# Sums on ScalarE, scores and exponentials in halves, and small norm steps shared anew in a transformer kernel on one core

## The chip, the cores and the metric

The kernel runs on one core of one Trainium2 chip. A core has five engines that run their own instruction queues and wait for each other on semaphores: TensorE (PE in the profile; PEld is its loading of weights), VectorE (DVE), ScalarE (ACT), GpSimd (POOL) and SyncE (SP), which here only starts transfers. The metric is the time of one execution on the device, in microseconds (us), lower is better. Before the change the median of three runs was 2978.14 us (2974.05 to 2979.39).

## The reference

The input `x` is 32 sequences of 128 tokens with 128 features, with a context of the same size. First comes a cross-attention of 16 query heads and 4 key heads of size 8 with a time bias, then six layers, each of a local attention and a gated feed-forward part. Cut to what matters here:

```python
# cross-attention, once
x = x + xattn(layernorm(x), ctx, ...)          # softmax over 128 keys, 16 heads

for i in range(6):
    # local attention: 16 heads of 64, windows of 32 tokens that see themselves and the window before
    t = shift_tokens(x)                         # second half of the features from the token before
    q, k, v = split(t @ Wqkv[i])
    q = l2norm(q) * q_scale[i]; k = l2norm(k) * k_scale[i]
    q, k = rotate(q), rotate(k)                 # rotary tables with a scale
    sim = (bq @ bk2) * 8, masked                # 32 queries x 64 keys per window
    x = softmax(sim) @ bv2 @ Wo[i] + x
    # feed-forward
    t = shift_tokens(x)
    n = (t - mean) / sqrt(var + 1e-5) * g + b
    a, gate = split(n @ W1[i] + b1[i])          # 341 each
    x = (a * gelu(gate)) @ W2[i] + b2[i] + x
```

All of it is float32. The values and the output projection are folded into one matrix per head.

## The kernel before, in words

Tokens lie on the 128 partitions. Work is cut into *units* of one sequence (32 per layer) and *groups* of four sequences (8 per layer, `GB = 4`); the residual of a group stays in SBUF in `xt0` to `xt7`. `xgroup` and `xunit` do the cross-attention, `prep` prepares a layer's weights, `lgroup` starts a group of a layer, `unit` does its attention and `ffn` its feed-forward part.

The order of the instructions is not the order of the code. Every step is an operation given to `Sched.op` with a name, an engine, the buffers that it reads and writes, and a priority. `Sched.run` plans all of them ahead, before the program is written: it books each engine for the time that the table `COST` gives the name (engine, time that it occupies the engine, time until its result is there), moves priorities by the table `LATER`, keeps some buffers back by `KEEP`, and takes, on each engine, the first ready operation in order of priority. The order that comes out is written into the five queues and is fixed; on the chip each engine then runs its queue in that order and waits where an operand isn't there yet. A change in any entry of these tables reorders the whole program.

One `unit` runs like this, with the names in the plan and the lines of the profile:

- `qk` (four operations): query and key projections on TensorE. Each is three matmuls of 128x512 (`split3`, L438 to L440), the product of high and low parts in the faster float32 form. They go to one of five PSUM banks (pool `pj`).
- `sq` (L786, ScalarE) squares and `ss` (L801, VectorE) sums for the norms; `tab` (L792, VectorE) multiplies by the rotary tables and `add` (L798, GpSimd) completes the rotation.
- `newton` makes the reciprocal square roots of 32 norms: `mxs` (L405, GpSimd) puts a floor under the sums, `ln` and `ep` (L408, L411, ScalarE) take exp(-0.5 ln v), `ysq` (L415, ScalarE) squares it, and three steps `nw` on GpSimd (L420, L423, L426) refine it: times v, times -0.5 plus 1.5, times y. The same function serves the layer norm (`eps`, `lnf`, `epf`, `nwf`).
- `mul` (L815, GpSimd) scales, `tq` (L444, TensorE) transposes, `evq` (L820, ScalarE) copies the transposed heads to `qT`, four buffers per unit: two of queries and two of keys.
- `msk` (L857, ScalarE) puts the mask into the two PSUM banks of scores; `sc` (L852, TensorE) adds all scores of the unit, 128 small matmuls, as one operation. Bank 0 holds the even heads, bank 1 the odd ones.
- `mx` (L865, VectorE) takes maxima. For bank 1 `fold` (L867, TensorE) adds the negative maximum and `ex` (L869, ScalarE) is one exponential over 512 columns. For bank 0 `exb` (L873, ScalarE) is eight exponentials of 64 columns, each with its maximum as the bias.
- For both banks `sm` (L875, VectorE) sums the probabilities, `rl` (L876) takes the reciprocal, `pl` (L877, GpSimd) scales, `pt` (L879, VectorE) transposes in blocks.
- `y`, `yt` and `dm` (L831 to L834) make the projected values and move them into shape by a transfer; `av` (L892, TensorE, 56 matmuls) multiplies probabilities with them.

In `ffn`, `res` (L900) adds, `shift` moves token halves by two transfers, `st` and `ag` (L906, L910) take mean and variance, `newton` the reciprocal root, `nmr` (L915, VectorE, a scalar_tensor_tensor over 128x4) makes minus mean times the root, and `xn` (L920, ScalarE) normalizes. `ptn`, three `gate`, three `pa`, `w2` (L956) are TensorE's; `gel` (L937) needs another table on ScalarE, which is loaded for each group and loaded back (L254).

Ahead of the plan stands a start written by hand (L300 to L383): loads of constants and weights on the queues of SyncE and ScalarE, fills on GpSimd, and a few operations.

Of the kernel before, what the change touches and what calls it, by code (L numbers as in the profile page):

```python
# [16 lines left out]
P = 128  # L17
# [13 lines left out]
    qk=("PE", 0.76, 0.95), sq=("ACT", 0.53, 0.63), ss=("DVE", 0.6, 0.68), tab=("DVE", 1.14, 1.22), add=("POOL", 1.27, 1.3), ta=("DVE", .63, .72), adda=("POOL", 1.1, 6),  # L31
    mxs=("POOL", 0.25, 0.29), dmx=("DVE", 0.4, 0.48), dnw=("DVE", 0.34, 0.42), ln=("ACT", .2, .24), ep=("ACT", .2, .24), nw=("POOL", 0.24, 0.27),
    mul=("POOL", 1.01, 1.06), tq=("PE", 0.44, 0.68), evq=("ACT", 0.51, 0.61), evk=("ACT", .5, .62),
    y=("PE", 0.76, 0.95), yt=("ACT", 0.52, 0.62), dm=("SP", 0.58, 7.0), xph=("ACT", .6, .7), xpl=("ACT", .6, .7), dw=("SP", .62, 3.5), dr=("SP", .62, 4.5),
    msk=("ACT", 0.54, 0.63), sc0=("PE", .52, .75), sc1=("PE", .52, .75), mx=("DVE", 0.6, 0.68), fold=("PE", 0.31, 0.5), ex=("ACT", .51, .62), exb=("ACT", 1.62, 1.72),
    sm=("DVE", 0.6, 0.68), rl=("DVE", 0.13, 0.21), pl=("POOL", 1.02, 1.06), pt=("DVE", 0.62, 0.7), av=("PE", 1.95, 2.05), sc=("PE", 1.46, 1.6),
    res=("DVE", .63, .72), psh=("SP", 1.65, 3.5), st=("DVE", 0.79, 0.87), ag=("DVE", .35, .40), xn1=("POOL", 1.08, 1.1),
    eps=("POOL", .22, .26), lnf=("ACT", .22, .21), epf=("ACT", .22, .21), nwf=("POOL", 0.18, 0.24), xn=("ACT", 1.55, 1.65), nmr=("DVE", 0.4, 0.48), ysq=("ACT", .2, .24), xn2=("POOL", 1.08, 1.1),
    ptn=("PE", .46, .70), xnh=("ACT", .51, .62), xnl=("DVE", .60, .66), gate=("PE", 0.75, 0.95), gel=("ACT", 0.63, 0.7),
    pa=("PE", 0.73, 0.94), um=("DVE", 0.68, 0.76), w2=("PE", .67, .90), res2=("DVE", .63, .72), xo=("POOL", 1.3, 1.3),  # L40
    io=("SP", .62, 3.5), ldw=("SP", 0.5, 4.0),
# [10 lines left out]
LATER = dict(y=-0.75, xsc=-0.25, evk=-0.25, axl=-3.15, tab0=-2.45, tq3=2.8, pv=2.6, sq2=0.2, xex=1.55, ss1=1.2,  # L52
    mul3=-0.25, rl0=4.45, bip=-2.55, add3=3.2, pl0=0.8, bid=-0.4, ss2=-0.85, sq1=-0.9, xpa=0.25, tq2=1.45, mx0=3.2,
    sq3=0.45, wvp=2.75, ax=-0.7, qk3=-0.5, qk=-1.45, yt3=-1.55, tab2=-0.85, ysq=0.55, tq1=0.5, gate2=-3.4, um=-1.5,
    add2=2.2, w1c=0.35, fold1=1.5, gate=-0.25, mul2=2.55, dnw=-1.1, fold0=-2.5, y3=3, exb0=6.15, axh=0.8, mp=-1.0,
    eps=-1.05, pl1=5.15, add0=1.5, xat=-1.65, tq0=-2.25, nwf=0.25, pt1=2.15, msk0=1.45, xn1=4.2, um0=0.3, y1=3.8,
    sq0=-0.5, evq0=0.25, add1=-0.25, mul0=0.25, mkb=4.25, qk1=-0.35, pa2=-2.3, qkh=-1.2, mxs=-2.4, yt2=1.3, yt1=1.45,
    tab1=-1.7, td=1, evq1=-1.95, lnb=-2.25, ep=0.6, ss0=3.1, add=-0.5, y0=2.9, gate1=0.2, pa1=0.6, exb=-1.55,
    xsb=-1.6, mul=3.3, gel2=-0.9, mul1=-2, tab=2.8, ex=0.35, gel1=-0.5, msk=-2.35, pa=-0.5, rl1=0.5, dm2=-1.5,
    ss=4.05, dm0=0.25, ag=1.5, xo=4, qk0=-0.3, ln=-1.75, evq=0.25, sq=1.35, pa0=0.35, xst=-0.95, vt=0.6, ss3=-0.75,  # L60
    hil=-0.55, st=-0.8, tb=3, um2=1.6, nmr=3.45, gel0=0.5, xrl=-0.75, xev=-1.75, gate0=-1.2, yt0=1.75, rl=1.5,
    dm3=-1.9, av=3.35, lof=-1, gel=0.75, xnh=1.6, pwm=-1.0, pl=-0.25, yt=-0.9, sm=-0.25, res2=-0.25, res=-0.5,
    tbm=0.8, ldw=-0.5, pt=-0.9, wve=-1, sm1=-0.5, fold=-1.25, w1a=0.75, dm1=-1.7, sm0=1, lnf=-2.75, w1b=0.25, epf=1.1,
    xag=-0.75, tq=1.5, sc=1.5, pt0=-1.05, evq2=0.1, qkl=4, xpj=-0.7, xmx=2, xrs=-0.75, mx=1, dm=1.9, ex1=0.25,
    um1=-0.25, ml=-2, y2=0.95, evq3=-0.75, w2=1.5, nw=-0.75)

KEEP = dict(qk=0, y=0, gate=0, pa=1, xtr=0, xpj=1, pv=1, td=1, xsc=0, wvp=2, mp=2, bip=2, sc0=0, tq=0, ptn=0, ax=0,
    w2=3)
# [167 lines left out]
def body(ctx: ExitStack, tc: tile.TileContext, x, ctx_in, fside, mask_in, xWq, xWk, xWv, xWo, xtw,  # L236
# [73 lines left out]
    xt = [tl(f"xt{g}", [P, GB, 192]) for g in range(NG)]  # L310
    us = [tl(f"us{i}_", [P, 512]) for i in range(2)]
# [38 lines left out]
    nc.sync.dma_start(fs[:B, :], fside)  # L350
    wl = S.pools["raw"][0][2](F32)[:, 0:2 * P].rearrange("p (a n) -> p a n", a=2)
    nc.sync.dma_start(wl[:, 0, :], xWq)
    nc.sync.dma_start(wl[:, 1, 0:32], xWk)
    tw = tl("tw", [P, 1])
    nc.sync.dma_start(tw, xtw.partition_broadcast(P))
# [18 lines left out]
    for t in xt:  # L374
        nc.gpsimd.memset(t[0:1, :, 128:192], 0.0)
# [16 lines left out]
    def newton(names, pri, V, src, n, floor, eps, pool_, cols):  # L392
        v, y, t = [Buf(p) for p in pool_]

        def sl(b):
            return b.t[:, 0:n]
# [4 lines left out]
        def f0():  # L401
            if eps is not None:
                e.tensor_scalar(sl(v), cols(), eps, None, op0=ALU.add)  # L403
            else:
                e.tensor_scalar(sl(v), cols(), floor, None, op0=ALU.max)  # L405

        def f1():
            nc.scalar.activation(sl(y), sl(v), AF.Ln)  # L408
# [22 lines left out]
        S.op(names[3], f4, pri, [t, v], [t])  # L431
        S.op(names[3], f5, pri, [t], [t])
# [340 lines left out]
    def unit(l, g, j, w, G, pri):  # L773
# [89 lines left out]
        def soft(a):  # L863
# [6 lines left out]
            else:  # L870
                def pieces():
                    for i in range(8):
                        nc.scalar.activation(r8(pr)[:, i], r8(s)[:, i], AF.Exp, bias=mx.t[:, i:i + 1].bitcast(F32))  # L873
# [169 lines left out]
```

## Time and profile before

| | us |
|---|---|
| median of three runs | 2978.14 |
| the profiled execution | 2981.35 |
| its span, first to last instruction | 2979.2 |
| TensorE busy | 2874.9 |
| VectorE busy | 2616.2 |
| GpSimd busy | 2590.3 |
| ScalarE busy | 2504.6 |

The granted clock of TensorE was 0.987 of full speed over the span. A row of the timeline gives start, duration, engine, line, operation and tiles; durations on one engine overlap a little, so the time that an instruction takes from its engine is read from start to start. A wait names the engine that released it as far as the semaphores show it; "issue" stands where they show nothing. The first score matmul of a layer stands at 295 us; what is ahead of it is the cross-attention and the first preparations. The last matmul stands at about 2973 us.

### The profile page before, as it was taken

To read this page: it belongs to the slowest core of one execution; us is meant where nothing else is said; L and a number is where in the kernel's file an instruction comes from. 1 tells how busy PE (TensorE), PEld (TensorE's weight loads), DVE (VectorE), ACT (ScalarE), POOL (GpSimd) and SP (SyncE) were. 2 spreads that over 40 slices of the span, in tenths; PEclk is the share of its full clock that TensorE was granted. 3 is DMA by queue.
4 is the path that set the end of the run, shared out by engine and by line. 5 is a ranking of instruction groups with operands and counts; after the bars stand their busy time and mean duration, and the time that the engine had idled before them with its cause. 6 is when DMAs were issued, how large, how long until landed. Compare 5 with 4: busy or idle time off the path is not lost.

```text
span 2979.2 us, 115523 instructions
## 1 busy us (share of the span) xinstructions
PE 2874.9 (96%) x47695; PEld 2301.4 (77%) x47695; DVE 2616.2 (88%) x5203; ACT 2504.6 (84%) x6143; POOL 2590.3 (87%) x3238
## 2 busy tenths in 40 slices
PE   8999999999999999999999999999999999999997
PEld 5666777787877887777877888877788887777775
DVE  6778989998989998888998999988999998889884
ACT  6888888888888987888888888988888888888885
POOL 7768999898988998888988999989889998889893
PEclk8999999999999999999999999999999999999999
DMA  4101565656555565645556655556556556456555
GB/s 115 37 14 30 95 91 80 90 79 104 94 78 88 81 92 99 91 74 81 93 78 110 93 80 90 79 86 112 84 81 93 80 89 100 73 91 95 82 89 76
DMA packets 216881, 250.77 MB, mean 84 GB/s; under 512 B 90622, under 2 KB 111394, under 8 KB 216354
## 3 DMA queue, kind: packets, MB, share of 16 engines
q1 hardware_dynamic: 215922, 243.04, 51.5%
q8 instruction: 375, 6.14, 1.2%
q14 instruction: 152, 1.25, 0.2%
q10 hardware_dynamic: 432, 0.34, 0.0%
HBM read 25.31 MB, written 4.19 MB: 10 GB/s over the span
## 4 chain that ended last, share of the span: by engine, by line
PE 80%; DVE 6%; POOL 5%; ACT 4%; issue 4%; DMA 1%; POOLq 0%; SPq 0%; DVEq 0%; ACTq 0%
PE bank__68 L892 11%; PE bank__66 L852 4%; PE bank__67 L852 3%; PE bank__64 L438 3%; PE bank__62 L444 3%; PE bank__61 L444 3%; PE bank__63 L438 3%; PE bank__63 L444 3%; PE bank__65 L438 3%; PE bank__62 L438 3%; PE bank__65 L444 3%; PE bank__61 L438 3%; PE bank__64 L444 3%; PE bank__64 L439 3%; PE bank__64 L440 3%
## 5 line engine op out<-in xcount | busy, mean ns | idle before, releaser
L857 ACT COPY bank__66<-mask 128x512 f32<-128x512 f32 x192 | 123.6, 644 | 6.0 <-PE bank__66 L371 4.7
L857 ACT COPY bank__67<-mask 128x512 f32<-128x512 f32 x192 | 124.9, 651 | 0.9 <-PE bank__67 L371 0.9
L254 ACT ACT_TABLE_LOAD x48 | 61.6, 1283 | 0.9
L937 ACT ACT_TABLE_LOAD x48 | 61.6, 1283 | 0.9
L723 ACT ACTIVATE ysh__88<-ysh__88 128x512 f32<-128x512 f32 x64 | 40.1, 643 | 7.4 <-POOL ysh__88 L721 7.0
L900 DVE TENSOR_TENSOR xt<-bank__68,xt 128x512 f32<-128x512 f32 x48 | 32.8, 684 | 5.5 <-PE bank__68 L892 5.3
L723 ACT ACTIVATE wch__89<-wch__89 128x512 f32<-128x512 f32 x16 | 10.3, 646 | 8.0 <-POOL wch__89 L721 7.9
L960 DVE TENSOR_TENSOR xt<-bank__62,xt 128x512 f32<-128x512 f32 x11 | 7.6, 687 | 10.5 <-PE bank__62 L956 10.3
L960 DVE TENSOR_TENSOR xt<-bank__64,xt 128x512 f32<-128x512 f32 x9 | 6.2, 692 | 10.4 <-PE bank__64 L956 10.1
L960 DVE TENSOR_TENSOR xt<-bank__65,xt 128x512 f32<-128x512 f32 x12 | 8.3, 691 | 6.0 <-PE bank__65 L956 5.7
L967 POOL TENSOR_TENSOR raw__50871<-raw__50871,xt 128x512 f32<-128x512 f32 x1 | 1.3, 1261 | 14.0 <-DVE xt L960 14.0
L960 DVE TENSOR_TENSOR xt<-bank__63,xt 128x512 f32<-128x512 f32 x10 | 6.9, 688 | 7.5 <-PE bank__63 L956 7.3
L723 ACT ACTIVATE wch__90<-wch__90 128x512 f32<-128x512 f32 x16 | 10.1, 634 | 1.9 <-POOL wch__90 L721 1.9
L444 PE MATMUL bank__62<-cs,ysh__88 128*128 128x128 f32 x56 | 9.8, 302 | 0.6 <-ACT ysh__88 L723 0.6
L723 ACT ACTIVATE wch__92<-wch__92 128x512 f32<-128x512 f32 x16 | 10.2, 639 | 0.0
L723 ACT ACTIVATE wch__91<-wch__91 128x512 f32<-128x512 f32 x16 | 10.1, 633 | 0.0
L694 DVE TENSOR_TENSOR xt<-bank__68,xt 128x512 f32<-128x512 f32 x8 | 5.5, 685 | 4.9 <-PE bank__68 L692 4.9
L726 ACT COPY ysh__88<-bank__62 128x512 f32<-128x512 f32 x14 | 8.4, 599 | 1.6 <-PE bank__62 L444 1.6
L444 PEld LDWEIGHTS bank__62<-cs,ysh__88 128*128 128x128 f32 x56 | 6.7, 152 | 3.9 <-issue 1.7
L408 ACT ACTIVATE ny__51731<-nv__51729 128x4 f32<-128x4 f32 x1 | 0.2, 206 | 11.3 <-POOL nv__51729 L403 11.3
L444 PE MATMUL bank__61<-cs,xt 128*128 128x128 f32 x64 | 9.6, 273 | 0.0
L444 PE MATMUL bank__63<-cs,ysh__88 128*128 128x128 f32 x52 | 8.8, 295 | 0.4 <-ACT xh__1332 L766 0.2
(24257 smaller groups left out, 15643.2 us busy)
## 6 DMA issues: line engine op xcount, KB each, us to landing
xt<-xt SPq DMA_DIRECT2D x96, 112.0 KB
xt<-in_x SPq DMA_DIRECT2D x16, 128.0 KB
x_scratch<-xt SPq DMA_DIRECT2D x8, 256.0 KB
xt<-xt SPq DMA_DIRECT2D x96, 15.0 KB
stg__690<-in_L_ffn_Wo SPq DMA_DIRECT2D x1, 512.0 KB
stg__6126<-in_L_ffn_Wo SPq DMA_DIRECT2D x1, 512.0 KB
stg__19159<-in_L_ffn_Wo SPq DMA_DIRECT2D x1, 512.0 KB
stg__27202<-in_L_ffn_Wo SPq DMA_DIRECT2D x1, 512.0 KB
```

The source lines that it names most:

```text
L254: S.back = lambda: nc.scalar.preload_act_table_set("natural_log_exp_and_others")
L438: nc.tensor.matmul(pt, lh, rh, start=True, stop=False)
L439: nc.tensor.matmul(pt, lh, rl, start=False, stop=False)
L440: nc.tensor.matmul(pt, ll, rh, start=False, stop=True)
L444: nc.tensor.transpose(dst[:, k * P:(k + 1) * P], srcs[k], ident if eye is None else eye)
L723: S.op("xex", lambda: nc.scalar.activation(sm.t, sm.t, AF.Exp), pri, [sm], [sm], table="E")
L852: nc.tensor.matmul(s4[a][32 * c:32 * c + 32, half, wd, lo:64], q[r, c * P + 32 * wd:c * P + 32 * wd + 32], k[r, c * P + 32 * wd - 32 + lo: ...
L857: S.op("msk", lambda b=b: nc.scalar.copy(b.t, mask), pri, (), [b], k=a)
L892: nc.tensor.matmul(po.t[32 * wd:32 * wd + 32, j * P:(j + 1) * P], p5[a][:, half, wd, blk, :], ysh[0].t[:, u * 512 + h * P:u * 512 + (h + 1 ...
L900: S.op("res", lambda: nc.vector.tensor_tensor(xv(g), hv(po.t), xv(g), op=ALU.add), pri, [po, X[g]], [X[g]])
L937: S.op("gel", lambda: nc.scalar.activation(u.t[0:n], pg.t[0:n], AF.Gelu, bias=b1c.t[0:n, 1, i:i + 1]), pri, [pg, b1c], [u], table="G", k=i)
L960: S.op("res2", lambda: nc.vector.tensor_tensor(xv(g), hv(py.t), xv(g), op=ALU.add), pri, [py, X[g]], [X[g]])
```

## The change

- `soft`: for bank 0, each of the eight exponentials also writes the sum of its 64 probabilities (`accum_out`), and the operation `exb` becomes two of four pieces each; `sm` on VectorE stays for bank 1 alone.
- `scores`: the operation `sc` becomes two, one per half, each of 64 matmuls. The first needs `qT` 0 and 2, the second `qT` 1 and 3.
- `newton`, for the norms of the unit: `mxs` also multiplies by -0.5 and `ln` takes it back with its scale, so that after `ysq` and one `nw` step a single scalar_tensor_tensor `dnw` on VectorE, (t + 1.5) y over 128x32, takes the place of two steps on GpSimd.
- `ffn`: `nmr` goes to GpSimd, as two steps, `nmg` (times -1) and `nmr` (times the root).
- Start: the loads of `fside`, `Wq`, `Wk` and the weight of the time bias move from SyncE's queue to ScalarE's; the zeroing of `xt` on GpSimd stands ahead of the other fills; the load of `x` has a name of its own (`iox`) in the plan.
- `COST`, `LATER` and `KEEP` are new in many entries; the entries of changed or new operations are shown below.

```diff
@@ COST
-    ... qk=("PE", 0.76, 0.95) ... nw=("POOL", 0.24, 0.27) ... tq=("PE", 0.44, 0.68) ... y=("PE", 0.76, 0.95)
-    ... exb=("ACT", 1.62, 1.72) ... av=("PE", 1.95, 2.05), sc=("PE", 1.46, 1.6) ... nmr=("DVE", 0.4, 0.48)
+    ... qk=("PE", 0.72, 0.94) ... nw=("POOL", 0.31, 0.33) ... tq=("PE", 0.43, 0.66) ... y=("PE", 0.72, 0.94)
+    ... dnw=("DVE", 0.36, 0.44) ... exb=("ACT", 1.17, 1.3) ... av=("PE", 1.92, 2.02), sc=("PE", 0.72, 0.9)
+    ... nmr=("POOL", .18, .24), nmg=("POOL", .2, .26) ... iox=("SP", 1.1, 4.0)
@@ KEEP
-    pa=1, w2=3
+    pa=0, w2=0
@@ body, start
     xt = [tl(f"xt{g}", [P, GB, 192]) for g in range(NG)]
+    for t in xt:
+        nc.gpsimd.memset(t[0:1, :, 128:192], 0.0)
...
-    nc.sync.dma_start(fs[:B, :], fside)
+    nc.scalar.dma_start(fs[:B, :], fside)
...
-    nc.sync.dma_start(wl[:, 0, :], xWq)
-    nc.sync.dma_start(wl[:, 1, 0:32], xWk)
+    nc.scalar.dma_start(wl[:, 0, :], xWq)
+    nc.scalar.dma_start(wl[:, 1, 0:32], xWk)
...
-    nc.sync.dma_start(tw, xtw.partition_broadcast(P))
+    nc.scalar.dma_start(tw, xtw.partition_broadcast(P))
...
-    for t in xt:
-        nc.gpsimd.memset(t[0:1, :, 128:192], 0.0)
@@ newton
-                e.tensor_scalar(sl(v), cols(), floor, None, op0=ALU.max)
+                e.tensor_scalar(sl(v), cols(), floor, -0.5, op0=ALU.max, op1=ALU.mult)
...
-            nc.scalar.activation(sl(y), sl(v), AF.Ln)
+            nc.scalar.activation(sl(y), sl(v), AF.Ln, scale=-2.0 if big else 1.0)
...
         S.op(names[3], f4, pri, [t, v], [t])
+        if big:
+            S.op("dnw", lambda: nc.vector.scalar_tensor_tensor(sl(y), sl(t), 1.5, sl(y), op0=ALU.add, op1=ALU.mult), pri, [y, t], [y])
+            return y
@@ xgroup
-        S.op("io", lambda: halves(x, g, xo(g), False), base - 8, (), [X[g]])
+        S.op("iox", lambda: halves(x, g, xo(g), False), base - 8, (), [X[g]])
@@ unit
-        S.op("sc", scores, pri, [*qT, *sc], sc)
+        for half in range(2):
+            S.op("sc", lambda half=half: scores(half), pri, [qT[half], qT[2 + half], *sc], sc, k=half)
...
-                def pieces():
-                    for i in range(8):
-                        nc.scalar.activation(r8(pr)[:, i], r8(s)[:, i], AF.Exp, bias=mx.t[:, i:i + 1].bitcast(F32))
-                S.op("exb", pieces, pri, [mx, s], [pr], table="E", k=a)
-            S.op("sm", lambda: nc.vector.tensor_reduce(sm.t, r8(pr), axis=AX.X, op=ALU.add), pri, [pr], [sm], k=a)
+                def pieces(h):
+                    for i in range(4 * h, 4 * h + 4):
+                        nc.scalar.activation(r8(pr)[:, i], r8(s)[:, i], AF.Exp, bias=mx.t[:, i:i + 1].bitcast(F32),
+                                             accum_out=sm.t[:, i:i + 1])
+                for h in range(2):
+                    S.op("exb", lambda h=h: pieces(h), pri, [mx, s], [pr, sm], table="E", k=f"{a}{h}")
+            if a in FOLD:
+                S.op("sm", lambda: nc.vector.tensor_reduce(sm.t, r8(pr), axis=AX.X, op=ALU.add), pri, [pr], [sm], k=a)
@@ ffn
-        S.op("nmr", lambda: nc.vector.scalar_tensor_tensor(mv.t[:, :, 0], mv.t[:, :, 0], -1.0, r.t[:, 0:GB], op0=ALU.mult, op1=ALU.mult),
-             pri, [mv, r], [mv])
+        S.op("nmg", lambda: nc.gpsimd.tensor_scalar(mv.t[:, :, 0], mv.t[:, :, 0], -1.0, None, op0=ALU.mult), pri, [mv], [mv])
+        S.op("nmr", lambda: nc.gpsimd.tensor_tensor(mv.t[:, :, 0], mv.t[:, :, 0], r.t[:, 0:GB], op=ALU.mult), pri, [mv, r], [mv])
```

## The prediction

> **What bounds the kernel now.** I read the page first, then the windows by layer, then the waits of PE, then PE's timeline around a score block.
>
> ```profile
> span 2979.2 us, 115523 instructions
> ...
> PE 2874.9 (96%) x47695; PEld 2301.4 (77%) x47695; DVE 2616.2 (88%) x5203; ACT 2504.6 (84%) x6143; POOL 2590.3 (87%) x3238
> ...
> PE 80%; DVE 6%; POOL 5%; ACT 4%; issue 4%; DMA 1%; POOLq 0%; SPq 0%; DVEq 0%; ACTq 0%
> ```
>
> PE is busy for 96% of the span and carries 80% of the chain. The windows of two middle layers (span, busy PE, PEld, DVE, ACT, POOL) show that the helpers are close behind:
>
> ```profile
> 1186.00:1629.00 443.00, 428.04 (x7490) 349.55 (x7489) 396.64 (x643) 375.40 (x937) 391.94 (x487) 0.99 0.56 86
> 1629.00:2072.00 443.00, 437.25 (x7800) 356.02 (x7799) 408.11 (x658) 385.74 (x963) 403.02 (x501) 1.00 0.58 91
> ```
>
> PE's waits are small, and most name no releaser ("issue", in the middle of a row of ready matmuls); the largest inside the layers that do are single events of a microsecond:
>
> ```profile
> PE bank__68 L892 <- issue: 9.4, 15, 2.0
> ...
> PE bank__64 L956 <- issue: 6.4, 3, 3.6
> ...
> PE bank__67 L867 <- DVE mx__27187 L865: 1.4, 1, 1.4
> PE bank__62 L438 <- ACT yt__13943 L833: 1.3, 1, 1.3
> ```
>
> Busy time also hides what a change of work costs PE. In the timeline (start, duration), one projection (L438, L439, L440) follows another after 1511.10 - 1510.40 = 0.70 us. Next to transposes and scores it takes more:
>
> ```profile
> 1510.40 0.39 PE L438 MATMUL bank__64<-wch__19756,xh__24803 128*128 128x512 f32 x1
> ...
> 1511.10 0.40 PE L438 MATMUL bank__65<-wch__19765,xh__23812 128*128 128x512 f32 x1
> ...
> 1514.00 0.48 PE L438 MATMUL bank__63<-wch__11868,xh__24803 128*128 128x512 f32 x1
> ...
> 1514.88 0.21 PE L852 MATMUL bank__66<-qT__25698,qT__25669 64*32 64x32 f32 x1
> ...
> 1516.24 0.50 PE L438 MATMUL bank__62<-wch__19483,xh__24803 128*128 128x512 f32 x1
> ...
> 1517.04 0.60 PE L444 MATMUL bank__64<-cs,rt__25187 128*128 128x128 f32 x4
> ```
>
> The projection after transposes and before scores takes 0.88, the 128 score matmuls 1.36, the projection behind them 0.80. These prices repeat: sorting all starts on PE between 330 and 2880 us by kind of work and its two neighbours, the quarter point of "projection between projections" is 0.69, "after transposes" 0.78, "before scores" 0.78, "after scores" 0.80. Summed at these quarter points the work makes 2426 us; the stretch took 2548. Of the 122 us between them some 57 are the waits without releaser (PE's idle rows over the run), so **at most 65 us are waits for other engines**. That is all a better overlap can return there, besides the ends.
>
> **The change, step by step** (192 units of one sequence and layer, 48 groups of four; one unit takes (2975 - 295)/192 = 13.95 us).
>
> *Scores in halves.* No matmul is added, but in the built order the score blocks rise from 192 to 372: only 12 units keep their halves together. So PE changes work 180 times more. Price of one more block: its boundaries are 0.09 (before scores) and 0.10 (after) at projections, 0.08 to 0.13 at transposes; inside, the block takes 1.36 although its weight loads start within 1.17, so up to 0.17 drains once per block. From below: the boundaries alone, counted pair by pair in both orders with these prices (fewer projections now follow transposes or attention, which gives some back), make +31 us. From above: 180 x (0.19 + 0.17) = +65. I take **+45**, the middle, since the drain overlaps the next load partly. It lies on PE, so on the path.
>
> *How close the halves stand.* Between the last transposes that a half needs and the half itself, PE's order leaves this much other work (at the prices above): before, 1.75 us at the median; after, 1.07 for the second half. Transposes to scores needs about 0.42 (first eviction after its transposes start; median of the evictions that found ScalarE idle 0.69) + 0.60 (the eviction) + 0.2 (shortest gap eviction to scores) - 0.36 (the transposes themselves) = 0.86 to 1.13. So the second half waits whenever ScalarE is late: 0 to 0.25 us x 192 = 0 to +48. I take **+15**: the nearest rows (evictions that found ScalarE idle) only just fit. Behind a waiting half stand the other units' projections, all in PE's order.
>
> *ScalarE sums the even heads.* The reduce of L875 goes for one of two score banks: -192 x 0.60 (start to start) on VectorE, and its hop on the chain to the reciprocal. On ScalarE each of 1536 small exponentials writes a sum too:
>
> ```profile
> 1518.68 1.77 ACT L873 ACTIVATE pr__25915<-bank__66,mx__25892 128x64 f32<-128x64 f32 x8
> 1520.26 0.68 ACT L869 ACTIVATE pr__25939<-bank__67 128x512 f32<-128x512 f32 x1
> ```
>
> Eight pieces last 1.58, 0.197 each. What the sum adds isn't in this trace. From below 0; from above one more small instruction, 0.19 (L411, 128x32, start to start). The middle, 0.095, gives 8 x 0.095 = +0.76 a unit on ScalarE: 12.0 (13.85 less the idle rows before its instructions, 345 us over 188 units) becomes 12.8 of 13.95. Not on the path, but the evictions queue behind it. In pieces of four, other evictions can go between, which takes up to 0.8 off such a wait.
>
> *Small norm steps.* POOL loses two of four steps per unit (L423, L426: 0.25 and 0.29 start to start), 192 x 0.54 = -104, and gains two small ones per group, 48 x 0.4 = +19: -0.44 a unit. VectorE gets their place as one step with two SBUF inputs (dnw), and gives up nmr, of the same form. The rows of nmr say what that costs:
>
> ```profile
> 367.50 1.04 POOL L815 TENSOR_TENSOR rt__4859<-rt__4859,ry__5067 128x512 f32<-128x512 f32 x1
> ...
> 367.56 1.00 DVE L915 SCALAR_TENSOR_TENSOR nmv__5096<-nmv__5096,ny__5129 128x4 f32<-128x4 f32 x1
> ```
>
> It started just after a POOL instruction and ended with it (368.54, 368.56); of 48 such rows 42 last over 0.3 us, mean 0.80, the shortest 0.12. So dnw costs VectorE from 0.12 to 1.25 each (the longest POOL work, L798); I take 0.75 (nmr start to start): +144, against -115 for the reduce and -36 for nmr. **VectorE gains nothing.** Behind a blocked dnw stand the table products that free PE's banks; the four scalings of the unit on POOL wait for it, and in a quarter of the units POOL's order has only 0.2 us of work to put between, so about 0.2 of POOL's 0.44 comes back as waiting.
>
> The Trainium skill, "SBUF — State Buffer", section "Who interferes with whom", says that a VectorE instruction with two SBUF inputs contends with a GpSimd instruction that reads SBUF, and that whoever starts first holds the shared port for the whole instruction. The rows agree (1.00 beside POOL's 1.04). It speaks against dnw and for moving nmr; without it dnw would be 0.12 and VectorE 0.63 a unit lighter.
>
> What all this takes from PE's 65 us of waits: from above all of it (-65); from below nothing, or a loss if ScalarE's extra 0.76 counts more than POOL's net 0.24 (+20). POOL was the fullest helper and gets a little relief, ScalarE gets load: I take **-30**.
>
> *Start.* Four loads leave SyncE's queue for ScalarE's, whose issues (0.43 each) end before its first copy at 7.12; the zeroing of xt moves ahead of the other fills on POOL. Input rows could be asked for from about 1.2 instead of 4.68: at best -3.5; nothing, if the weights or the context then come last. I take **-3**. The cross-attention's order is new too, with the same blocks (75 runs of scores in both): 0, within 5 either way. The last 14 us are one chain of a group; minus and plus 0.2.
>
> Sum: 45 + 15 - 30 - 3 = +27 on the profiled execution's 2981.35, so 3008. That execution is 3.2 above the median of the runs (2978.14): 3005.
>
> **Rivals.**
> 1. *Faster: the waits on PE go.* The one mechanism is POOL: it is free for 0.44 us more per unit, so the rotated heads come earlier and PE finds its operands. For it: POOL is the fullest helper. Against: dnw hands the time back, and all waits are 65 us. Price: -65 (plus some -10 in the ends and the first 330 us), boundaries at their low end +31, start -3: -47, so 2931. It decides from the point where more than 55 of the 65 us go with boundaries at 45, or 35 with boundaries at 31.
> 2. *Slower by more: ScalarE or the second halves become the bound.* If the sum costs a whole small instruction, ScalarE reaches 12.0 + 1.5 = 13.5 of 13.95 and can't give evictions in time; or each second half waits 0.25. Boundaries 45 + 48 - 3, no relief: +90, so 3068.
> 3. *The parts cancel:* boundaries 31, waits -28, start -3: 2978.
> That the split isn't made is excluded: the order has 372 blocks.
>
> **How the numbers follow.** Forecast (2985 to 3030) 0.45; rival 2 (3030 to 3100) 0.16; rival 1 (2920 to 2970) 0.27; cancelling 0.12. No change is within 0.2% (6 us), about what a measurement can tell here. Slower: 0.45 + 0.16 = 0.61; of the cancelling case 0.11 stay within the 6 us and 0.01 falls below; faster 0.27 + 0.01 = 0.28. The likeliest is 3005, its own range 2985 to 3030. For 8 in 10 I go to 2945 below (leaving out a third of rival 1, 0.10) and 3060 above (half of rival 2, 0.08).
>
> **What would show it.** Boundaries: projections beside half blocks at 0.78 to 0.88 and half blocks near 0.7. VectorE busy not below 2600 and dnw near 0.8, ending with POOL's work. ScalarE's piece near 0.29. First statistics near 6 us instead of 9.60. I am wrong if PE's starts have fewer waits than 35 us in 330 to 2880, or if half blocks cost nothing at their edges.

## The result and the profile after

The changed kernel took **3067.64 us** (median of 4 runs, 3063.55 to 3070.35), the kernel before 2977.03 us beside it: a ratio of 1.0304, 95% interval 1.0286 to 1.0322. It is 90.6 us slower. The forecast was 3005, its range ended at 3060: right in sign, too low by two thirds of the loss, and the measured time lies above its range.

From the page of the changed kernel, its span, busy times and chain:

```profile
span 3065.6 us, 116691 instructions
...
PE 2917.4 (95%) x47695; PEld 2284.2 (75%) x47695; DVE 2564.3 (84%) x5155; ACT 2633.1 (86%) x7679; POOL 2537.7 (83%) x2950
...
PE 64%; DVE 12%; ACT 10%; POOL 6%; issue 3%; DMA 3%; SPq 0%; POOLq 0%; DVEq 0%; ACTq 0%
```

VectorE and GpSimd are each busy 52 us less than before and ScalarE 129 us more, but no helper is fuller than 86%. What changed is the chain: PE carried 80% of it and now 64%; VectorE's part has doubled and ScalarE's more than doubled. So PE waits more for results. In the stretch from 1629 to 2072 us PE is busy for 422.01 us and begins 7254 matmuls; before it was 437.25 and 7800, at the same granted clock of 1.00. (Over the whole span PE's busy time rose, from 2874.9 to 2917.4 us, though the durations of its rows sum to 12676 and 12665: the rows overlap less.) The waits of PE's weight loads, whose rows stand ahead of their matmuls, show new releasers: 4.7 us for L441 (four times, gelu L943 still reads the bank), single waits of 4.0 us for L447 (scaled heads, L818), 2.0 for L447 (eviction L823), 1.8 for L870 (maxima L868) and 2.4 for L898 (transposed probabilities, L885). Each is small; there are many. Summed over the layers of the profiled execution (from 35 us behind the first score block to 60 us ahead of the last, gaps over 0.15 us), the waits of PE's weight loads with a named releaser rose from 75 to 223 us, while those without one ("issue") fell from 200 to 145: 275 to 368, +92. The layers (first score block to last) took 2741 instead of 2646 us, +95; the start is 7.6 us shorter (first score block at 288.0 instead of 295.6).

That the two agree doesn't make the whole loss waiting. The weight loads' own busy time hardly moves (2301.4 us before, 2284.2 now), so whatever stretches PE's row stands between them as idle time, a change from one kind of matmul to another too. A half block of scores shows it:

```profile
1645.59 0.61 ACT L823 COPY qT__27410<-bank__63 128x512 f32<-128x512 f32 x1
...
1646.80 0.10 PEld L854 LDWEIGHTS bank__67<-qT__27410,qT__27395 64*32 64x32 f32 x1 [0.37 <-ACT sq__27429 L789]
```

The gap of 0.37 begins at 1646.43; the second of its two operands was there at 1646.20, and the squares named as the releaser are no operand of scores. Such a gap, 0.36 at the median, stands ahead of nearly every score block of both kernels: 191 gaps with 69 us before, 359 with 115 now.

The prediction's own method separates the two: price every step on PE by the quarter point of its times from start to start between the same two neighbours (here over both kernels' traces), and sum the prices over the sequence of the layers. **The price of PE's sequence rose from 2416 to 2469 us, +53; what the layers took beyond it rose from 134 to 177, +43.** (With the 5th or the 40th percentile in place of the quarter point: 55 and 42, 57 and 39; with prices from the traces of all kernels run here: 63 and 33.) So somewhat more than half of the loss is PE's own sequence, which changes work 180 times more, and the rest is waiting. Put down to the step that started late, the 43 are 19 ahead of folds, 12 ahead of transposes, 10 ahead of score blocks, 5 ahead of attention, and -3 in the others. The rest also holds the stops for which the profile shows no releaser; in PE's matmul rows they fell from 54 to 17 us, so the waits for named engines rose by more than 43.

Two edits as the trace shows them. ScalarE's sum is an instruction of its own, ACTIVATION_READ_ACCUMULATOR, behind each small exponential; a piece with its sum goes from start to start in 0.29 us instead of 0.20, as forecast. Here are two pieces in the first unit of the layers:

```profile
295.30 0.31 ACT L876 ACTIVATE pr__3968<-bank__66,mx__3950 128x64 f32<-128x64 f32 x1
...
295.50 0.20 ACT L876 ACTIVATION_READ_ACCUMULATOR pr__3968<-bank__66,mx__3950 128x1 f32 x1
295.59 0.31 ACT L876 ACTIVATE pr__3968<-bank__66,mx__3950 128x64 f32<-128x64 f32 x1
```

On PE, one half block of scores stands between two projections; 0.79 for the projection ahead of it, 0.74 for the half:

```profile
1646.01 0.39 PE L441 MATMUL bank__64<-wch__26773,xh__26646 128*128 128x512 f32 x1
...
1646.80 0.21 PE L854 MATMUL bank__67<-qT__27410,qT__27395 64*32 64x32 f32 x1
...
1647.54 0.50 PE L441 MATMUL bank__65<-wch__19718,xh__26646 128*128 128x512 f32 x1
```

The page's costliest groups on ScalarE are the copies of the mask, which still cost what they did, so its work as such isn't slower:

```profile
L859 ACT COPY bank__66<-mask 128x512 f32<-128x512 f32 x192 | 120.1, 626 | 5.4 <-DMA xt<-in_x 4.8
...
L859 ACT COPY bank__67<-mask 128x512 f32<-128x512 f32 x192 | 121.0, 630 | 1.5 <-PE bank__67 L373 1.1
```

They took a mean of 644 and 651 ns before, 626 and 630 now.

### The profile page after: what moved, and what is told of

Read it like the earlier page. It is cut to its first block, busy times and chain, and to the rows that moved or that the text cites. A ratio compares the mean times of both kernels' runs of the same rounds, so it can differ in the third digit from the quotient of the medians.

```text
span 3065.6 us, 116691 instructions
## 1 busy us (share of the span) xinstructions
PE 2917.4 (95%) x47695; PEld 2284.2 (75%) x47695; DVE 2564.3 (84%) x5155; ACT 2633.1 (86%) x7679; POOL 2537.7 (83%) x2950
## 4 chain that ended last, share of the span: by engine, by line
PE 64%; DVE 12%; ACT 10%; POOL 6%; issue 3%; DMA 3%; SPq 0%; POOLq 0%; DVEq 0%; ACTq 0%
PE bank__68 L898 9%; PE bank__66 L854 3%; PE bank__67 L854 3%; PE bank__64 L447 2%; PE bank__63 L447 2%; DMA xt<-xt 2%; PE bank__62 L447 2%; PE bank__61 L441 2%; PE bank__65 L441 2%; PE bank__62 L441 2%; PE bank__64 L441 2%; PE bank__63 L441 2%; PE bank__65 L447 2%; PE bank__61 L447 2%; PE bank__65 L443 2%
## 5 line engine op out<-in xcount | busy, mean ns | idle before, releaser
L859 ACT COPY bank__66<-mask 128x512 f32<-128x512 f32 x192 | 120.1, 626 | 5.4 <-DMA xt<-in_x 4.8
L859 ACT COPY bank__67<-mask 128x512 f32<-128x512 f32 x192 | 121.0, 630 | 1.5 <-PE bank__67 L373 1.1
L729 ACT COPY ysh__96<-bank__65 128x512 f32<-128x512 f32 x15 | 9.0, 598 | 2.8 <-PE bank__65 L447 2.3
L447 PE MATMUL bank__65<-cs,ysh__96 128*128 128x128 f32 x60 | 9.8, 288 | 0.8 <-ACT ysh__96 L726 0.7
L447 PE MATMUL bank__64<-cs,ysh__96 128*128 128x128 f32 x60 | 9.8, 288 | 0.1
L447 PEld LDWEIGHTS bank__65<-cs,ysh__96 128*128 128x128 f32 x60 | 7.0, 146 | 3.5 <-ACT ysh__96 L726 1.4
L447 PEld LDWEIGHTS bank__64<-cs,ysh__96 128*128 128x128 f32 x60 | 7.1, 146 | 3.4 <-ACT ysh__96 L726 2.4
L729 ACT COPY ysh__96<-bank__64 128x512 f32<-128x512 f32 x15 | 8.9, 596 | 0.7 <-PE bank__64 L447 0.7
```

The costliest lines, as they stand in the source:

```text
L447: nc.tensor.transpose(dst[:, k * P:(k + 1) * P], srcs[k], ident if eye is None else eye)
L729: S.op("xev", lambda: nc.scalar.copy(sm.t, pt.t), pri, [pt, sm], [sm])
L859: S.op("msk", lambda b=b: nc.scalar.copy(b.t, mask), pri, (), [b], k=a)
```

## The experiments

Differences are medians against the kernel before in the same job (2982 to 2984 us). Three theories stood first. A: the sums load ScalarE, and PE waits for its evictions. B: the new order, which the re-tuned tables make, leaves operands no time. C: dnw on VectorE is held by GpSimd.

### Single edits in the order of before

The sums alone, written to a spare tile, with VectorE's reduce kept (so their price without their gain; the cut `...` stands for the maxima):

```diff
-  nc.scalar.activation(r8(pr)[:, i], r8(s)[:, i], AF.Exp, bias=...)
+  nc.scalar.activation(r8(pr)[:, i], r8(s)[:, i], AF.Exp, bias=..., accum_out=spare[:, i:i + 1])
```

> The kernel before, in its own order, with each of the eight exponentials of the even heads also writing its sum, into a tile that nobody reads; VectorE's sums stay. Theory A (load on ScalarE: after the change each sum is an instruction of its own, 0.10 us start to start, 0.79 us a unit, and evictions come late for TensorE): a good part of the 90 us, 3020 to 3060. Theory B (the new order: the tables were re-tuned so that TensorE's operands come just in time): ScalarE had 1.84 us a unit free, so 2975 to 2995. Theory C (the norm step on VectorE, blocked by GpSimd): 2975 to 2990.

Measured 3029.21: **+46.9**, ratio 1.0155 (1.0139 to 1.0171). The page of this run:

```profile
PE 2896.1 (96%) x47695; PEld 2290.2 (76%) x47695; DVE 2618.5 (87%) x5203; ACT 2627.8 (87%) x7679; POOL 2598.5 (86%) x3238
...
PE 66%; ACT 12%; DVE 9%; issue 5%; POOL 5%; DMA 2%; SPq 0%; POOLq 0%; DVEq 0%; ACTq 0%
```

ScalarE is at 87% and yet its part of the chain goes from 4% to 12%.

dnw alone, in the place of GpSimd's last two steps (not shown: the factor -0.5 goes to `mxs`, and `ln` takes it back):

```diff
-  e.tensor_scalar(sl(t), sl(t), -0.5, 1.5, ...);  e.tensor_tensor(sl(y), sl(y), sl(t), op=ALU.mult)
+  nc.vector.scalar_tensor_tensor(sl(y), sl(t), 1.5, sl(y), op0=ALU.add, op1=ALU.mult)
```

> The kernel before, in its own order, with the two last norm steps of a unit on GpSimd replaced by the one step on VectorE, put where the second of them stood. A: VectorE gains 0.55 a unit, GpSimd loses as much: 2970 to 2990. B: the same. C: VectorE blocked for 0.55 a unit and the scalings late: 3010 to 3060.

Measured 2996.74: **+14.5** (1.0028 to 1.0063). The page of this run:

```profile
PE 2873.7 (96%) x47695; PEld 2295.5 (77%) x47695; DVE 2653.7 (89%) x5395; ACT 2515.4 (84%) x6143; POOL 2519.4 (84%) x2854
...
PE 61%; DVE 17%; POOL 8%; issue 6%; ACT 6%; DMA 1%; SPq 0%; POOLq 0%; DVEq 0%; ACTq 0%
```

GpSimd is 71 us lighter than before and VectorE 37 us heavier, but VectorE's part of the chain goes from 6% to 17%.

The start alone, with the layers' order unchanged:

```diff
+    for t in xt:  nc.gpsimd.memset(t[0:1, :, 128:192], 0.0)      # ahead of the other fills
-    nc.sync.dma_start(...)      # fs, wl (two), tw
+    nc.scalar.dma_start(...)
```

> The kernel before with the edits of the start alone: four constant loads on ScalarE's queue instead of SyncE's, the zeroing of xt ahead of the other fills; the layers' order is unchanged. The prediction gave this -3 (at best -3.5). The changed kernel reaches its first score matmul 7.6 us earlier than before (288.0 against 295.6), but there the cross-attention's order is new too. If the loads do it: 2973 to 2977 (-5 to -8.) If the earlier first scores came from the new order alone: 2980 to 2983, no change.

Measured 2983.44: ratio 1.0005 (0.9991 to 1.0019), **no change**. The first statistics did start at 6.56 instead of 9.60 us, but the first score block of the layers came at 295.1, almost as before (295.6): behind the cross-attention the gain is used up. So these edits alone don't give the 7.6 us of the changed kernel; its order there is another too.

The start and nmr in two steps on GpSimd:

```diff
-  nc.vector.scalar_tensor_tensor(mv0, mv0, -1.0, r, op0=ALU.mult, op1=ALU.mult)
+  nc.gpsimd.tensor_scalar(mv0, mv0, -1.0, None, op0=ALU.mult);  nc.gpsimd.tensor_tensor(mv0, mv0, r, op=ALU.mult)
```

> The kernel before with the edits of the start (which cost nothing, 2983.44 us) and nmr in two steps on GpSimd; the order is unchanged. If nmr on GpSimd is what was missing in the sum of the single edits (47 + 14 against 79): 2992 to 3005. If the edits act on each other when they come together: 2975 to 2988.

Measured 2997.62: **+14.0** (1.0034 to 1.0064), for 48 places. In the page GpSimd's part of the chain is 11% instead of 5%:

```profile
PE 2883.8 (96%) x47695; PEld 2301.0 (77%) x47695; DVE 2591.3 (86%) x5155; ACT 2504.6 (84%) x6143; POOL 2610.6 (87%) x3334
...
PE 68%; POOL 11%; DVE 7%; ACT 7%; issue 5%; DMA 2%; POOLq 0%; SPq 0%; DVEq 0%; ACTq 0%
```

### All of these together, in the order of before

> The order of before with every edit that it can take: sums on ScalarE (into a spare tile, the reduce kept), dnw on VectorE, nmr in two steps on GpSimd, the loads of the start. Score blocks stay whole. Theory L (the loss of the changed kernel is the load that the edits put on the helpers, in whatever order): the sum of the single runs, 47 + 14, less up to 7 for the start and with -10 to +5 for nmr, that is 2982 + 44 to 66, or more if the delays add up worse than singly: 3060 to 3080 would make it the whole loss. Theory O (much of the loss is that the changed kernel has another order, less well fitted): 3020 to 3048, so that 20 to 45 of the 86 us are left for the order with the halves.

Measured 3061.54: **+79.3** (1.0242 to 1.0280). The single edits sum to 47 + 14 + 14 = 75: they add up, and theory L holds for this order (VectorE's reduce of the even heads is kept here; the prediction put it at 115 us of VectorE's time). Its page:

```profile
span 3060.5 us, 116928 instructions
...
PE 2918.1 (95%) x47695; PEld 2295.3 (75%) x47695; DVE 2639.1 (86%) x5347; ACT 2633.6 (86%) x7679; POOL 2541.5 (83%) x2950
...
PE 46%; ACT 22%; DVE 16%; issue 7%; POOL 7%; DMA 1%; POOLq 0%; SPq 0%; DVEq 0%; ACTq 0%
```

PE's sequence costs as much as before here (+3 us); the layers' other 77 are waiting. The longest waits are those of the fold (here L872) behind the maxima (L870), up to 2.5 us. Between 330 and 2900 us all such fold waits sum to 41 us in 48 events, where before they were 7 us in 15. VectorE is hardly busier for it (2639 us, before 2616); its queue has dnw in it; that the score banks also reach it later from ScalarE is likely, but not shown. So a loss nearly as large appears without the changed kernel's order and without halves, but it is made of waits alone.

### The changed order without the loads

The changed kernel without the sums (the even heads stay unnormalized):

> The changed kernel in its own order without the sums on ScalarE; the reciprocal of the even heads is replaced by a small VectorE instruction on one column of the probabilities, so their normalization is left out. A: most of the loss goes, 2985 to 3020. B: 3045 to 3065, since the order is as tight as it was. C: 3055 to 3070.

Measured 3056.95: +74.7 (1.0230 to 1.0267).

The same, and dnw made an operation with one SBUF input:

> The changed kernel's order with both loads taken away: ScalarE writes no sums, and dnw is an operation with one SBUF input that no GpSimd work can hold (the even heads' normalization and the Newton step are left out, so its results are other numbers). Without the sums alone it took 3056.95. Theory L (load): with both away 2985 to 3010. Theory O (the order): 3035 to 3057, that is, at least 50 of the 86 us remain though the helpers have less to do than in the kernel before.

Measured 3045.93: **+63.7** (1.0192 to 1.0228). So sums and dnw, which cost 61 us in the old order, give back 27 in the new one, and 64 stay without them (nmr is still on GpSimd). Its page:

```profile
PE 2911.0 (96%) x47695; PEld 2287.0 (75%) x47695; DVE 2516.2 (83%) x5155; ACT 2515.9 (83%) x6143; POOL 2530.6 (83%) x2950
...
PE 71%; DVE 8%; POOL 7%; ACT 6%; issue 4%; DMA 3%; SPq 0%; POOLq 0%; DVEq 0%; ACTq 0%
```

No helper is fuller here than in the kernel before, where they were at 84 to 88% (ScalarE is busy 11 us longer, VectorE 100 and GpSimd 60 us less), and VectorE and ScalarE still take more of the chain than there (6% and 4%). Both theories are half right, and **the two parts don't add**: loads alone 79, the order nearly alone 64, both 91. In the layers of this run 53 us are the price of PE's sequence, which is that of the changed kernel, and 21 are waiting (changed kernel: 43).

Lighter helpers in the changed order, first VectorE alone:

```diff
-  nc.vector.tensor_reduce(ss..., sq.t.rearrange("p (h d) -> p h d", d=64), ...)
+  nc.vector.tensor_reduce(ss..., sq.t.rearrange("p (h d) -> p h d", d=64)[:, :, 0:32], ...)
```

> The changed kernel's order; the reduce of the squares (ss) sums only half of each head's columns, four times a unit (the norm of q and k is then another number). VectorE becomes about 4 x 0.28 = 1.1 us a unit lighter, and the statistics come earlier. If the order waits for VectorE above all (its share of the chain is the largest after PE's, 12%): 2990 to 3030. If the waits lie with all helpers alike, as much per us of work as the sums gave back on ScalarE (11 us for 0.76 a unit): 3045 to 3060.

Measured 3060.51: +78.6 (1.0234 to 1.0310). It isn't VectorE above all.

Then three helpers (half of the reduce on VectorE, half of the heads' scaling on GpSimd, no sums on ScalarE):

> The changed kernel's order with three helpers lightened: no sums on ScalarE (-0.76 us a unit), half of the squares' reduce on VectorE (-1.1), half of the scaling of the rotated heads on GpSimd (-2.0). Left out: the even heads' normalization and half of two other steps. If the 64 to 85 us that the order loses are waits for helpers: 2930 to 2990, since PE's own work per unit is no larger than in before. If PE's order itself is at fault (gaps that no faster helper closes, such as the distance between the second half and its transposes): 3030 to 3050.

Measured 3028.53: **+46.6** (1.0128 to 1.0195), just under the second expectation and far above the first. Its page:

```profile
PE 2913.4 (96%) x47695; PEld 2294.2 (76%) x47695; DVE 2367.4 (78%) x5155; ACT 2514.1 (83%) x6143; POOL 2218.9 (73%) x2950
...
PE 79%; DVE 7%; ACT 6%; issue 3%; DMA 3%; POOL 1%; SPq 0%; POOLq 0%; DVEq 0%; ACTq 0%
```

With VectorE at 78% and GpSimd at 73%, PE's part of the chain is back at 79%, but half of the loss is still there. It is no longer more waiting than before: what the layers took beyond the price of PE's sequence is 139 us here, 134 before, and the sequence costs 52 more. **Lighter helpers take back the waits; what stays is the longer sequence on PE.**

### Is it the tables?

The work of before, planned with all three new tables, with the new costs, with the new keep-rows, and with the new delays and keep-rows:

```diff
-LATER = dict(y=-0.75, xsc=-0.25, ...)      +LATER = dict(y=-0.35, iox=1.8, ...)
-KEEP = dict(..., pa=1, ..., w2=3)          +KEEP = dict(..., pa=0, ..., w2=0)
-COST: qk 0.76, sc 1.46, gate 0.75, ...     +COST: qk 0.72, sc 1.44, gate 0.72, ...
```

> The work of the kernel before (whole scores, whole exponentials, sums on VectorE, norm steps on GpSimd), planned with the new tables of costs, delays and kept buffers, the four changed operations booked as they are here. A and C: the tables alone are worth little, 2960 to 3000. B: the tables carry the loss, 3030 to 3090.

> The work of before, planned with before's delays and keep-rows, but with the changed kernel's costs (score block 1.44, small exponentials 1.62, as that work has them). The order of before with all three tables new took 3077.57 us, 95 above before. Theory B1 (the delays, LATER, carry the loss): the costs differ by 0.02 to 0.07 a step, so 2975 to 3000 here. Theory B2 (the costs carry it, because PE is planned 5% tighter): 3040 to 3080. Theory B3 (the tables fit one another, and any mixture loses, whichever part is exchanged): above 3010 here, and also in the two runs beside it.

> The work of before with before's costs and delays, and the changed kernel's keep-rows (the up-projection pa and the second matmul w2 no longer hold back for others: pa 1 to 0, w2 3 to 0). Theory B1 (delays): 2975 to 3000, since only where those matmuls stand may change. Theory B4 (keep-rows carry the loss): 3040 to 3080. Theory B3 (any mixture loses): above 3010.

> The work of before with before's costs, and the changed kernel's delays and keep-rows. Theory B1 (delays): 3050 to 3090, all of the 95 us that the three new tables cost. Theory B2 (costs): 2975 to 3010. Theory B3 (any mixture loses): above 3010, and then also in the run with the costs alone.

Measured: all three 3077.57 (**+95.3**), costs 3045.49 (**+63.4**), keep-rows 3059.89 (**+77.8**), delays and keep-rows 3046.56 (**+64.4**), each within 7 us either way. The chain of the run with the new keep-rows alone shows what happens to a work that is the same to the last instruction:

```profile
PE 2897.9 (95%) x47695; PEld 2295.4 (75%) x47695; DVE 2600.0 (85%) x5203; ACT 2503.8 (82%) x6143; POOL 2588.7 (85%) x3238
...
PE 59%; DVE 18%; ACT 8%; POOL 6%; issue 4%; DMA 4%; SPq 0%; POOLq 0%; DVEq 0%; ACTq 0%
```

VectorE and ScalarE are busy as before in us, and carry 26% of the chain, not 10%. PE's sequence costs as before in all four (-8 to +7 us), so these losses are waiting. No table carries the loss: B1, B2 and B4 would each need a harmless neighbour, and there is none, though the delays alone were not run. B3 holds. The other way round, the changed kernel's work with before's costs and delays (the keep-rows stay the new ones):

> All edits of the changed kernel (half score blocks, sums on ScalarE, dnw on VectorE, the loads), planned with before's costs and delays; the keep-rows are the new ones, and the rows that only the edits need (halves 0.73, pieces of four 1.17, the new norm steps) are the new ones too. Theory B (the new tables lose, the edits much less): 2990 to 3045, that is, below the changed kernel by 20 to 75, as the sums (+47) and dnw (+14) cost what they did in the order of before, less the 7 us of the earlier start. Theory A (the edits lose by ScalarE's load in any order, and the new tables are the best answer to them): 3065 or more. If it ends below 2975, the edits win by themselves and the new tables alone lose.

Measured 3140.41 (**+158.3**): a miss of theory B, which expected at most 3045. The new tables are not bad in themselves; they are worth 68 us to the changed work (158 against 91). In these runs a table is worth something only with the work that it was fitted to.

A slight change of the plan:

```diff
-rl=("DVE", 0.13, 0.21)
+rl=("DVE", 0.14, 0.22)
```

> The kernel before with a single planned cost raised by 0.01 us (the reciprocal rl, 0.13 to 0.14); the work is the same, the planner makes another order from the second layer on. If the order of before is a peak that any new planning leaves: 3020 to 3060, as with the new costs (3045) or keep-rows (3060). If slight changes of the plan are harmless and the tables of the change lose by something of their own: 2975 to 2995.

Measured 2983.40: 1.0005 (0.9988 to 1.0021), no change. But in this plan 3710 of PE's 3930 steps keep their place in the queue (counted in the built orders); with the new keep-rows 1351 do, with the new costs 1174. So it shows that small shifts are harmless, not that a wholly new order can be; and not every change of an entry reorders the whole program.

### The halves and the banks

The first half moved to stand directly before the second in the changed order (the two emitted together, where no tile is taken anew between), which joins 106 of 180 split blocks:

> The changed kernel with its order kept, but the first half of the scores moved on PE to stand directly before the second, wherever none of its tiles is taken anew in between (106 fewer score blocks in the layers, 266 instead of 372). The prediction's boundaries (45 us for 180 more blocks, from 31 to 65): 106 joined give back 26 (18 to 38), so 3030 to 3050. If, as the trace of the changed kernel says, half blocks cost nothing at their edges: 3060 to 3075. Above 3080 if the first half was useful as work for PE while the second half's operands come.

Measured 3080.04: +97.8 (1.0306 to 1.0351), 7 us more than the changed kernel loses, not 26 less; the intervals of the two overlap a little. The joined blocks did give back what they were priced at: PE's sequence costs 2445 us instead of 2469, 24 less. But what the layers took beyond it rose from 177 to 223 (in an execution 11 us above this run's median). A half that is ready early is useful work for PE.

Halves alone, in the work of before with the new keep-rows:

> The work of before with the scores in halves and nothing else of the change, planned with before's costs (0.73 a half) and delays and the new keep-rows (with the old ones the plan cannot be finished). The fair neighbour is the same kernel with whole blocks, 3059.89 us. If halves lose by themselves: above 3080. If they gain: below 3045. Between: the halves do nothing that the new planning does not.

Measured 3075.92: +94.0, which is 16 more than its neighbour with whole blocks (3059.89), with 191 more blocks. The sequence costs 49 us more than the neighbour's (2458, 2408) and the waiting is 33 less (190, 223): the halves cost PE their boundaries and give it work for times in which it would wait, in orders that differ anyway.

Last, a count in the built orders: how often PE comes back to a bank of its pool of five with less than 1.5 us of its own work since the last use. It is 470 before and 649 in the changed kernel. So the changed kernel was planned with a margin:

```diff
-  k = [s for s in self.pools[p] if s[0] is not None and s[0] + lat <= t]
+  k = [s for s in self.pools[p] if s[0] is not None and s[0] + lat + (0.6 if p == "pj" else 0) <= t]
```

> The changed kernel with all its edits and tables, but the planner takes a bank of the pool of five only 0.6 us after it expects it free. In the built order PE comes back to a bank with less than 1.5 us of its own work in between 571 times instead of 649 (before: 470), with less than 1.2 us 315 times instead of 388 (before: 353). If the late evictions of banks are what the new order loses by: 3020 to 3052. If it is something else that new orders have in common: 3055 to 3090, no better than the changed kernel (3067).

Measured 3096.89: **+113** (1.0368 to 1.0403). The theory falls: with fewer short returns (571) the layers take as long (2744 us, changed kernel 2741), and as much of it is waiting (+46, +43). The 29 us by which the run is slower than the changed kernel lie ahead of them: the first score block comes at 317.1 us instead of 288.0. The chain of this run has the parts of the changed kernel's:

```profile
PE 2950.3 (95%) x47695; PEld 2321.1 (75%) x47695; DVE 2547.5 (82%) x5155; ACT 2640.8 (85%) x7679; POOL 2536.9 (82%) x2950
...
PE 66%; DVE 13%; ACT 9%; POOL 7%; issue 4%; DMA 2%; SPq 0%; POOLq 0%; DVEq 0%; ACTq 0%
```

### What all runs have in common

Layers is the time from the first score block to the last; waits are those of PE's weight loads in it, summed from the records; price is that of PE's sequence and rest what the layers took beyond it, both against before (us, one profiled execution each):

| | layers | waits with releaser | "issue" | all waits, against before | price | rest | layers, against before |
|---|---|---|---|---|---|---|---|
| before | 2646 | 75 | 200 | | | | |
| start alone | 2645 | 74 | 203 | +2 | 0 | -1 | -1 |
| start and nmr | 2660 | 81 | 209 | +15 | 0 | +14 | +14 |
| dnw alone | 2657 | 109 | 185 | +19 | 0 | +10 | +11 |
| sums alone | 2691 | 122 | 213 | +60 | +1 | +44 | +45 |
| all edits, old order | 2725 | 161 | 209 | +95 | +3 | +77 | +79 |
| **changed kernel** | 2741 | 223 | 145 | +92 | +53 | +43 | +95 |
| its order, no loads | 2719 | 193 | 150 | +68 | +53 | +21 | +73 |
| its order, three helpers light | 2700 | 170 | 153 | +48 | +52 | +5 | +54 |
| halves joined | 2762 | 212 | 171 | +109 | +29 | +89 | +116 |
| old work, new tables | 2741 | 175 | 186 | +86 | +7 | +89 | +95 |
| new work, old tables | 2816 | 277 | 150 | +152 | +55 | +114 | +170 |
| old work, new keep-rows | 2725 | 167 | 195 | +87 | -8 | +89 | +79 |
| the same with halves | 2741 | 200 | 155 | +80 | +41 | +56 | +95 |
| bank margin | 2744 | 190 | 154 | +70 | +53 | +46 | +98 |

In each row but the last the waits and the layers agree within 18 us, whatever the cause; that sum can't tell a boundary from a late result. The prices can: orders with whole blocks cost PE what the order of before did (-8 to +7 us), orders with halves 41 to 55 more, the joined one 29, with the same 47695 matmuls in all. What is left, the rest, moves with the loads and with how well plan and work fit.

## Why the prediction was wrong

**The failing step is "what all this takes from PE's waits", booked at -30** (-65 to +20). With second halves (+15) the prediction had PE's waiting fall by 15; it rose by 43, of which 10 stand ahead of score blocks, so +33 stands in the place of the -30. It took GpSimd's relief for what PE waits for, because GpSimd was the fullest helper. In the old order the edits that this step covers cost +75 one by one and +79 together. Three reasons:

- *"Not on the path, but the evictions queue behind it."* The sum's size was right (0.29 a piece; 0.75 a unit), its price was not booked: 1536 x 0.094 = 144 us of ScalarE's time cost 47 us of the kernel's in the old order, 0.3 for each. The bound "if ScalarE's extra counts more" should have been a share of its 144 us, not 20.
- *dnw.* Booked 0.75, measured 0.55 (mean of 192 rows; median 0.41, longest 1.56). VectorE's busy time ended at 2564, where the text said not below 2600: 192 x 0.2 = 40 us. Alone it is still a loss of 14, with VectorE's part of the chain up from 6% to 17%; that the delay of the unit's chain counts and not VectorE's sum is likely. The held rows look as in the rows of nmr; of the 92 that last over 0.5 us, 90 end within 0.15 us of a GpSimd instruction that started before them. One beside a product of GpSimd:

```profile
376.71 1.06 POOL L883 TENSOR_TENSOR pr__5335<-pr__5335,sm__5344 128x512 f32<-128x512 f32 x1
...
376.80 1.02 DVE L433 SCALAR_TENSOR_TENSOR ry__5236<-rw__5339,ry__5236 128x32 f32<-128x32 f32 x1 [0.51 <-POOL rw__5339 L420]
```

It starts 0.09 behind GpSimd's work and ends 0.05 behind it. This agrees with the Trainium skill, "SBUF — State Buffer", section "Who interferes with whom", that whoever starts first holds the shared port for the whole instruction.

- *nmr to GpSimd* was counted as relief for VectorE (-36). Alone it costs 14 us: two steps behind GpSimd's long products in place of one, in the chain that starts each feed-forward group.

**Boundaries, +45 (31 to 65): right**, +53 by the prediction's own method. Two halves cost 1.47 where the whole block cost 1.36; a projection ahead of a block costs 0.79, one behind it 0.80, one among its like 0.69 (the shortest of these rows lie within 0.05 of the quarter points). The run with the joined halves returned 24 for 106 blocks, as priced, and lost more in waits.

**Second halves, +15 (0 to +48):** right, +10. The idle time of weight loads ahead of score blocks rose by 46 us, but most of that is the gap that stands ahead of every block.

**Start, -3: wrong, it is 0** (-3 to +6). **Cross-attention, 0 within 5:** the layers came forward by 7.6, more than that. Together: 53 + 43 - 8 = 88; the profiled executions differ by 3067.40 - 2981.35 = 86.

**The rivals.** Rival 1 (waits go) is excluded: they rose in every kernel that had any of the edits of the layers. Rival 2 gave 3068, and 3067.64 was measured. Its sum comes near too (boundaries 45, measured 53; no relief but 48 of waiting, measured 43; -3, measured -8), though that the total agrees within 1 us is luck. Its two conditions didn't come: ScalarE's pieces are 0.29, not 0.39, and the second halves hold PE for 10 us, not 48; most of the waiting stands ahead of folds and transposes. Its chance of 0.16 was too small. In rival 1 one figure is off: with boundaries at 45 it decides from some 50 of the 65 us (45 - 3 - 50 = -8, the edge of its 2970), not 55. Of the signs named in the prediction, projections beside half blocks at 0.79 and 0.80, half blocks near 0.7, pieces near 0.29 and statistics near 6 us (6.42) came true; VectorE not below 2600 and dnw near 0.8 didn't.

**What stays open.** Nothing was booked for a wholly new order. Four such orders of before's work lost 63 to 95 us, all in waiting, and the changed order without its loads still waits 21 us longer than before. The runs exclude the costs or the keep-rows alone, VectorE alone and the short returns to a bank as the one cause. Why folds and transposes get their operands late in one plan and not in another, and whether a plan of the changed work exists that does better than 3067, they don't show. None of the kernels run here is faster than the one before.

## What to carry to other kernels

When the bound engine is busy for 96% and the helpers for 84 to 88%, price work moved to a helper by what a late result does to the bound engine's queue: here 144 us of ScalarE's time cost 47, and 48 small steps moved cost 14, although no helper was full. Where a step of the bound engine is split, price the added changes of work in its own row: 180 of them cost 53 us here, and 41 to 55 in every plan with halves, while the waits depended on the plan. Where a planner makes the order, treat a new plan as a change with its own price, which the diff doesn't show, and measure the edits in the old order first. Sum the bound engine's sequence at undisturbed prices before you call its idle time waiting: here the waits of its weight loads followed the loss in nearly every run, and more than half of the changed kernel's loss was hidden in them.

## What was not expected of the hardware

- The accumulating output of a small exponential is a separate instruction, 0.22 us long at the median; a piece of 128x64 with it takes 0.29 from start to start, without it 0.20.
- The waits of PE without a releaser are not fixed: 200 us in the weight loads before, 145 after, with the same matmuls; in the matmul rows themselves 54 and 17. Why they fall isn't shown.
- Splitting a block of 128 small matmuls in two between 128x512 matmuls costs PE about 0.3 us each time (0.11 in the block, 0.10 and 0.11 at the neighbours), though no matmul is added.
